# Moving products, a gate and half the stores around in an attention and convolution kernel

## The chip, the core and the metric

The kernel runs on one core of a Trainium2 chip. The metric is the device time of one execution in microseconds, the median over runs. The core has five engines that run side by side, each with its own queue of instructions in a fixed order, and wait for each other by semaphores: TensorE (PE in the profile; its weight loads are shown apart as PEld), VectorE (DVE), ScalarE (ACT), GpSimd (POOL), and SyncE (SP), which only issues DMAs. Matmul results land in PSUM, [...] from which DVE and ACT copy them to SBUF.

## What is computed

The input `x` has 8 images of 64 channels and 64 x 64 pixels. Layer 0 is attention over the 4096 pixels of each image, with an added global (unary) term; layer 1 sums three convolutions (1x1, 3x3, 5x5) of signs with sign weights, each with a batch norm, and multiplies the sum by a gate that is computed from its mean:

```python
# layer 0
q = wq @ xf + bq;  k = wk @ xf + bk;  v = wv @ xf + bv
q = q - q.mean();  k = k - k.mean()          # over the pixels
sim = softmax(q.T @ k / 8)                   # 4096 x 4096 per image
x = x + v @ sim.T + v @ softmax(q_mean @ k)
# layer 1
s = sum(norm_k(conv_k(sign(x + move_k), sign_weights_k)) for k in (1, 3, 5))
gate = sigmoid(grouped(mean(s)) + gb)        # one number per image and channel
out = s * gate + x
```

## The kernel before

Two images form a pair, one on partitions 0 to 63, one on 64 to 127; there are four pairs. Their 4096 queries are cut into NQ = 8 blocks of 512. I call block g the g-th of the 32 blocks; g // 8 is its pair and qb = g % 8 its place in the pair. Each block walks over the 4096 keys in 32 steps of 128 (`attend`, L1057 to L1068). The order of all instructions is written out by hand: what Python calls first stands first in the queue of its engine.

One step j does this. `scores` (L466) issues four f32 matmuls of 64 x 64 x 512 to a score tile `ps` (a pair of banks; the pool has two such tiles, tag "s"), and ACT takes the exponential into a tile `e` (L481). Then, for the step before, `weighted` (L484) multiplies those exponentials by the values and adds into `acc` (one pair of banks, tag "acc"), and `summed` (L497) has DVE add them into `es`, the denominators. After that come the pieces of other work that `plan` (L953) put at step j with `put`; pieces at the same step run in the order of the `put` calls.

At step 0 of a block, between the last weighted sums of the block before and the first ones of the new block, lies what I call the seam. There `weighted_out` (L506) copies `acc` to SBUF (tile `o`), `send` and `gather` (L516, L523) carry `es` through DRAM into a tile `parts` from the pool of exponentials, and `both` (L982) calls `mix_rows` (L862). That function interleaves two sequences of small matmuls, one for each half of the array's rows: the queries of block g + 1 (`pq`, two halves in two "m" banks), and the convolutions of block g - 3. Those are 70 products for the 5x5 (groups S, A, B in one score tile, D in an "m" bank), 24 for the 3x3 (A, B, S, D in the pair of banks "acc") and two 1x1 matmuls. Each entry of a sequence has a length in units (queries 2.0, a product 0.5, the 1x1 1.0), and the two sequences are merged by running position; each entry issues two matmuls. When the queries' matmuls are done, `split_queries_out` (L459) moves them to SBUF; when 5x5 D is done, `begin_rows` (L700) has ACT start the sum tile `sb` from it. At the end `hold_rows` (L729) has ACT copy the 3x3 results to SBUF (`es_z`), and `add_rows` (L715) has DVE add S (two additions), A and B of the 5x5 to `sb`. The held 3x3 results and the 1x1 are added some steps later (`add_held`, `end_rows`).

`fold` (L531) turns the gathered `parts` into reciprocals `rec`, and `spread` (L543) sends them through DRAM to all partitions. `check_block` lets ACT compare them with limits. `added` and `finish` make the layer's output `x2` on DVE, and the `signs` functions put its signs into padded images on ACT.

Once per pair there is more. The next pair's `x` is loaded in its predecessor's block qb = 2; `mean_part` sums it (DVE, quarters), `mean_scores` at block qb = 4 makes from it, with a one-column matmul `pm`, the vectors `mx` and `nmx` that the queries need; `values` and `unary_part` follow in qb = 4 to 7; `unary_end` at the next pair's block 0 has two one-column matmuls `po`. The gate of a pair takes `gate_mean` and `gate` (a one-column matmul `pg`, then ACT and DVE), and `store` multiplies a block of sums by it on DVE and sends it out.

## Time and profile before

| | us |
|---|---|
| median of 3 runs | 1955.12 (1954.63 to 1955.45) |
| the profiled execution, whole | 1956.16 |
| its span in the profile | 1953.9 |
| mean granted TensorE clock | 0.998 |
| ACT exponentials, L481, 1024 of them | 1049.1 busy, 1.025 each |
| DVE additions to `es`, L504, 960 of them | 1173.2 busy, 1.222 each |
| TensorE scores, L470, 8192 records | 1094.8 busy |
| TensorE weighted sums, L489, 8192 records | 1086.7 busy |
| DVE `fold`, L533, 31 of them | 60.7 busy, 1.958 each |

Busy time of TensorE counts the time in which at least one matmul runs; four 64 x 64 matmuls can run at once in the four quarters of the array, and each f32 matmul leaves two records. In the chain that ended last, four such matmuls of 512 columns take 0.86 us together. L12 is line 12 of the kernel. A record such as "L481 ACT ACTIVATE e<-ps" names the line, the engine, the operation, and the tile written and read.

### The profile page before, as it was taken

The page shows a single profiled execution, that of the slowest core. Times are in us where ns is not written, and L with a number is a line of the kernel's source. Part 1 is how long each engine was busy: PE and PEld are TensorE (multiplying, and loading weights), DVE is VectorE, ACT ScalarE, POOL GpSimd, SP SyncE. Part 2 cuts the span into 40 slices and gives each one's busy share as a digit, 9 for nine tenths or more (in the row PEclk, how much of TensorE's full clock was granted, in tenths as well). Part 3 has the DMA queues.
Part 4 walks back from the last instruction along what each step waited for, and adds up shares of the span by engine and source line. Part 5 has one row for each costly group of instructions (what it writes and reads, how often), then busy time and mean ns, then how long its engine had stood idle before and what let it go on. Part 6 is the DMA issues. An engine that isn't in the chain of part 4 may idle for free.

```text
span 1953.9 us, 48347 instructions
## 1 busy us (share of the span) xinstructions
PE 1927.4 (99%) x20848; PEld 810.3 (41%) x20848; DVE 1683.2 (86%) x2077; ACT 1249.1 (64%) x1474; POOL 5.9 (0%) x26
## 2 busy tenths in 40 slices
PE   9999999999999999999999999999999999999997
PEld 4333434443444434444444443344444444444444
DVE  6878988889888899888898888998888888988976
ACT  5666666666666666666666666666666666666663
POOL 0000000000000000000000000000000000000000
PEclk9999999999999999999999999999999999999999
DMA  3021111110102121111101212011111011111111
GB/s 100 31 69 30 27 37 34 40 35 16 40 31 83 37 67 29 37 34 40 34 16 40 74 50 67 20 36 37 34 39 33 17 40 52 62 39 33 28 34 46
DMA packets 58997, 80.57 MB, mean 41 GB/s; under 512 B 15628, under 2 KB 40600, under 8 KB 58648
## 3 DMA queue, kind: packets, MB, share of 16 engines
q1 hardware_dynamic: 58024, 76.22, 12.8%
q8 instruction: 165, 2.70, 0.6%
q10 hardware_dynamic: 720, 1.18, 0.2%
q14 instruction: 56, 0.46, 0.1%
q0 software_dynamic: 32, 0.01, 0.0%
HBM read 39.27 MB, written 24.77 MB: 33 GB/s over the span
## 4 chain that ended last, share of the span: by engine, by line
PE 87%; DVE 6%; ACT 5%; issue 1%; DMA 1%; SPq 0%; DVEq 0%; ACTq 0%
PE acc L489 41%; PE ps L470 40%; DVE es L504 4%; PE z L692 2%; ACT sb L707 1%; ACT es_z L732 1%; ACT e L481 1%; PE pq L455 1%; PE pv L311 1%; PE z L763 1%; DMA e_parts<-es 1%; PE z_5d L692 0%; DVE fold L533 0%; DMA x<-in_x 0%; DVE sb L725 0%
## 5 line engine op out<-in xcount | busy, mean ns | idle before, releaser
L481 ACT ACTIVATE e<-ps 128x1024 f32<-128x1024 f32 x1024 | 1049.1, 1025 | 623.9 <-PE ps L470 584.4
L504 DVE TENSOR_TENSOR es<-es,e 128x1024 f32<-128x1024 f32 x960 | 1173.2, 1222 | 137.9 <-ACT e L481 85.1
L470 PE MATMUL ps<-q,x 64*64 64x512 f32 x8192 | 1094.8, 591 | 0.9 <-DVE kb L165 0.9
L489 PE MATMUL acc<-e,v 64*64 64x512 f32 x8192 | 1086.7, 590 | 7.6 <-ACT e L481 4.6
L489 PEld LDWEIGHTS acc<-e,v 64*64 64x64 f32 x8192 | 325.7, 131 | 570.5 <-ACT e L481 297.6
L470 PEld LDWEIGHTS ps<-q,x 64*64 64x64 f32 x8192 | 348.7, 133 | 501.0 <-issue 271.4
L725 DVE SCALAR_TENSOR_TENSOR sb<-z,frac,sb 128x256 f32<-128x256 f32 x87 | 39.2, 478 | 61.8 <-PE z L692 61.8
L692 PE MATMUL z<-e,wt 64*64 64x256 bf16 x754 | 84.3, 269 | 0.1
L692 PE MATMUL z<-ec,wt 64*64 64x256 bf16 x754 | 84.3, 270 | 0.0
L692 PEld LDWEIGHTS <-wt 64*64 64x64 bf16 x1508 | 76.7, 105 | 1.1 <-issue 0.3
L692 PEld LDWEIGHTS <-wc 64*64 64x64 bf16 x1218 | 67.5, 105 | 2.9 <-issue 0.5
L533 DVE TENSOR_REDUCE fold<-e_parts 128x256 f32<-128x1024 f32 x31 | 60.7, 1958 | 3.6 <-DMA e_parts<-es 3.6
L725 DVE SCALAR_TENSOR_TENSOR sb<-es_z,frac,sb 128x256 f32<-128x256 f32 x145 | 62.2, 479 | 0.0
L692 PE MATMUL z<-ec,wc 64*64 64x256 bf16 x464 | 60.9, 271 | 0.0
L707 ACT ACTIVATE sb<-z_5d,shift,frac 128x256 f32<-128x256 f32 x58 | 29.6, 561 | 41.1 <-PE z_5d L692 41.1
L608 ACT ACTIVATE s<-x,vec 128x512 bf16<-128x512 f32 (+2 forms) x66 | 46.2, 702 | 5.4 <-DVE x L576 5.2
L502 DVE TENSOR_TENSOR es<-e,e 128x1024 f32<-128x1024 f32 x32 | 39.2, 1225 | 8.6 <-ACT e L481 8.6
L692 PE MATMUL z<-e,wc 64*64 64x256 bf16 x319 | 44.8, 271 | 0.0
L462 DVE TENSOR_SCALAR q<-pq,mx 128x256 f32<-128x256 f32 x60 | 27.0, 480 | 15.5 <-PE pq L455 15.0
L511 ACT COPY o<-acc 128x1024 f32<-128x1024 f32 (+2 forms) x33 | 32.3, 981 | 1.2 <-PE acc L489 1.2
L311 PEld LDWEIGHTS pv<-wx,x 64*64 64x64 f32 x1024 | 22.3, 134 | 17.1 <-issue 8.8
L732 ACT COPY es_z<-z 128x1024 f32<-128x1024 f32 x29 | 29.3, 1011 | 0.0
(153 smaller groups left out, 713.8 us busy)
## 6 DMA issues: line engine op xcount, KB each, us to landing
es<-es SPq DMA_DIRECT2D x31, 512.0 KB
e_parts<-es SPq DMA_DIRECT2D x124, 128.0 KB
r<-rc SPq DMA_DIRECT2D x62, 128.0 KB
x<-in_x SPq DMA_DIRECT2D x15, 512.0 KB
out<-sb SPq DMA_DIRECT2D x28, 256.0 KB
ec<-e SPq DMA_DIRECT2D x29, 153.0 KB
xc<-in_x SPq DMA_DIRECT2D x60, 64.0 KB
ec<-e SPq DMA_DIRECT2D x29, 132.0 KB
```

Of the source, the lines that this page charges most:

```text
L311: nc.tensor.matmul(pv[img[h], b, i * w : (i + 1) * w], self.x[img[b], bass.ds((4 * g + i) * P + h * H, H)], self.wx[img[b], :], start=True ...
L470: nc.tensor.matmul(ps[img[h], b, :], self.x[img[b], bass.ds(j * P + h * H, H)], self.q[qb][img[b], :], start=True, stop=neg is None,)
L481: nc.scalar.activation(e, ps, AF.Exp, scale=1.0 / 8.0)
L489: nc.tensor.matmul(self.acc[qb][img[b], h, :], self.v[img[h], j, img[b]], e[img[h], b, :], start=(j == 0), stop=(j == NK - 1),)
L502: nc.vector.tensor_tensor(self.es[qb], self.first, e, ALU.add)
L504: nc.vector.tensor_tensor(self.es[qb], self.es[qb], e, ALU.add)
L533: nc.vector.tensor_reduce(f, self.parts.rearrange("p g c -> p c g"), AX.X, ALU.add)
L608: nc.scalar.activation(sy[n][0][:, rows, pad : pad + HH], self.x2[qb][:, r0 * HH : r1 * HH].rearrange("p (h w) -> p h w", w=HH), AF.Sign, ...
L692: nc.tensor.matmul(z[img[b], :].rearrange("p (h w) -> p h w", w=HH), taps[img[h], c * C : c * C + C], src[:, first : first + 3 * step + 1 ...
L707: nc.scalar.activation(sv[:, :, t, :], z.rearrange("p (j w) -> p j w", w=HH), AF.Identity, bias=shift, scale=frac[5][:, t : t + 1],)
L725: nc.vector.scalar_tensor_tensor(out, z.rearrange("p (j w) -> p j w", w=HH), by, out, ALU.mult, ALU.add)
L732: nc.scalar.copy(self.z3, two)
```

## The change

- In `mix_rows` the order of the products changes. Before, the first sequence was 5x5 S, 3x3 A, the 1x1, 3x3 B, S, D, and the second 5x5 A, D, B. Now the first is eight of S, all 3x3, the last two of S, the 1x1, and the second six of A, all D, the last four of A, B. `hold_rows` is called when 3x3 D is done, no longer after all products.
- `both` is put ahead of `mean_scores`, `unary_end` and `mean_rows_out` at step 0.
- Half the queries' results go to SBUF on ACT in place of DVE.
- `gate` moves from step 0 of block qb = 3 to step 13 of qb = 2, `gate_mean` from step 20 to 11; four of the eight `store` calls of a pair move to block qb = 2, and the others start at step 12 of qb = 3 with 4 steps between them, in place of step 3 with 3 between.
- The means of the next pair are taken in eight parts on ACT in place of four on DVE.
- `fold` is cut into `fold_first`, `fold` and `fold_last` at steps 3, 4, 5: two additions of halves in place of one reduction over four. `spread`, `add_held`, `end_rows`, `added` and `finish` move one to four steps later.
- The pool of exponentials (and `parts`) has five buffers in place of four. Room comes from smaller scratch tiles, the tile `rc` used for the fold too, and nine sum tiles `sb` in place of ten.

```diff
-    ep = ctx.enter_context(tc.tile_pool(name="ep", bufs=4))
+    ep = ctx.enter_context(tc.tile_pool(name="ep", bufs=5))
...
-                junk = ep.tile([P, N // 4], F32, tag="e", name=f"mean_{self.name}_{c}")
+                junk = sm.tile([P, N // 4], BF16, tag="cl", name=f"mean_{self.name}_{c}")
...
-            for h, c in enumerate(SPLIT):
-                nc.vector.tensor_scalar(
-                    q[:, c], self.pq[h][:, 0 : c.stop - c.start], self.mx, None, ALU.subtract
-                )
+            data = [self.pq[h][:, 0 : c.stop - c.start] for h, c in enumerate(SPLIT)]
+            nc.vector.tensor_scalar(q[:, SPLIT[0]], data[0], self.mx, None, ALU.subtract)
+            nc.scalar.activation(q[:, SPLIT[1]], data[1], AF.Identity, bias=self.nmx)
...
+        def fold_first(self, qb):
+            two = [self.parts[:, 2 * i : 2 * i + 2, :] for i in range(2)]
+            nc.vector.tensor_tensor(two[0], two[0], two[1], ALU.add)
+            self.rc = self.tile(fp, "rc", qb, (P, QB // 2))
+
         def fold(self, qb):
-            f, t = self.tile(fp, "fold", qb, (P, QB // 2)), self.parts[:, 0, :]
-            nc.vector.tensor_reduce(f, self.parts.rearrange("p g c -> p c g"), AX.X, ALU.add)
+            parts, f, t = self.parts, self.rc, self.parts[:, 0, :]
+            nc.vector.tensor_tensor(f, parts[:, 0, :], parts[:, 1, :], ALU.add)
             nc.vector.transpose(out=t, in_=f)
+
+        def fold_last(self, qb):
+            t = self.parts[:, 0, :]
             nc.vector.tensor_reduce(
                 rec, t.rearrange("p (k i) -> p k i", i=32), AX.X, ALU.add
             )
             nc.vector.reciprocal(rec, rec)
...
+        def sum_tile(self, qb):
+            return bp.tile([P, QB], F32, tag="sb", bufs=9, name=f"sb_{self.name}_{qb}")
...
-            seqs[0] += products(5, "S") + products(3, "A") + [((1,), 0, 1.0)]
-            seqs[0] += products(3, "B") + products(3, "S") + products(3, "D")
-            seqs[1] += products(5, "A") + products(5, "D") + products(5, "B")
+            S, A = products(5, "S"), products(5, "A")
+            three = [t for name in "ABSD" for t in products(3, name)]
+            seqs[0] += S[:8] + three + S[8:] + [((1,), 0, 1.0)]
+            seqs[1] += A[:6] + products(5, "D") + A[6:] + products(5, "B")
...
+            elif left[n] == 0 and n == (3, "D"):
+                p.hold_rows(qb, z3)
         if c is not None:
-            p.hold_rows(qb, z3)
             for n in "SAB":
                 p.add_rows(qb, 5, n, z[5, n])
...
-            if qb == 3 and pr >= 1:
-                put(0, pairs[pr - 1].gate)
+            put(0, both)
             if qb == 4 and pr + 1 < n_pairs:
-                put(0, lambda: nx().mean_scores())
+                put(0, lambda: nx().mean_scores(8))
...
-            put(0, both)
             if g >= 3:
                 p3, b3 = block(g - 3)
-                put(4, p3.add_held, b3, "AB")
-                put(6, p3.add_held, b3, "SD")
-                put(8, p3.end_rows, b3)
+                put(7, p3.add_held, b3, "AB")
+                put(8, p3.add_held, b3, "S")
+                put(9, p3.add_held, b3, "D")
+                put(10, p3.end_rows, b3)
             if g >= 1:
-                put(3, p.fold, b)
-                put(5, p.spread, b)
+                put(3, p.fold_first, b)
+                put(4, p.fold, b)
+                put(5, p.fold_last, b)
+                put(6, p.spread, b)
...
-                put(10, p.added, b)
-                put(12, p.finish, b)
+                put(12, p.added, b)
+                put(13, p.finish, b)
...
-                put(20, pairs[pr - 1].gate_mean)
-            if qb == 3 and pr >= 1:
-                for i in range(NQ):
-                    put(3 + 3 * i, pairs[pr - 1].store, i, rows_of(pr - 1))
+                put(11, pairs[pr - 1].gate_mean)
+                put(13, pairs[pr - 1].gate)
+            if qb in (2, 3) and pr >= 1:
+                for i in range(NQ // 2):
+                    put((15, 12)[qb - 2] + 4 * i, pairs[pr - 1].store, NQ // 2 * (qb - 2) + i, rows_of(pr - 1))
...
-                    for c in range(4):
-                        put(14 + 4 * c, lambda c=c: nx().mean_part(c, quarters[c]))
+                    for c in range(8):
+                        cols = slice(c * QB, (c + 1) * QB)
+                        put(14 + 2 * c, lambda c=c, cols=cols: nx().mean_part(c, cols, True))
```

## The prediction

> **What bounds the kernel now.** I read the page first, then the order of instructions in time at one ordinary seam (the stretch between two blocks, step 0 of a block), then the waits, then the starts of all 1024 exponentials.

> From the page, busy time and the chain that ended last:

> ```profile
> PE 1927.4 (99%) x20848; PEld 810.3 (41%) x20848; DVE 1683.2 (86%) x2077; ACT 1249.1 (64%) x1474; POOL 5.9 (0%) x26
> ...
> PE 87%; DVE 6%; ACT 5%; issue 1%; DMA 1%; SPq 0%; DVEq 0%; ACTq 0%
> ```

> TensorE is the bound. In mid-block nothing else shows: exponentials start every 1.717 us (605.58, 607.30, 609.01), which is the 0.86 us of scores plus 0.86 us of weighted sums in the chain. So what the change can win are the places where an exponential starts later than 1.717 us after the one before. A plain block takes 58.58 us (1028.57 to 1087.15): 32 x 1.717 = 54.95, and 3.63 at its seam. Blocks with two `values` take 1.02 more (59.60), TensorE's own work. Beyond these: block 1 (58.35 us, with no convolution in its seam), block 2 (57.42, likewise), block 4 (62.83, so 3.23 extra), blocks 11, 19, 27 (61.25, 2.67 extra), 12 and 20 (61.11, 1.51 extra), 8, 16, 24 (59.83, 1.25 extra). The ends of these blocks are in step; nothing else is lost but start and tail, which the change leaves alone.

> The seam of block 10 in order of time (start, length, engine, line; in brackets the idle time before and who ended it):

> ```profile
> 609.93 1.01 ACT L511 COPY o<-acc 128x1024 f32<-128x1024 f32 x1
> ...
> 610.28 0.88 DVE L462 TENSOR_SCALAR q<-pq,mx 128x256 f32<-128x256 f32 x2 [0.70 <-PE pq L455]
> ...
> 611.97 1.02 ACT L707 ACTIVATE sb<-z_5d,shift,frac 128x256 f32<-128x256 f32 x2 [1.03 <-PE z_5d L692]
> ...
> 612.93 1.01 ACT L732 COPY es_z<-z 128x1024 f32<-128x1024 f32 x1
> 613.14 0.88 DVE L725 SCALAR_TENSOR_TENSOR sb<-z,frac,sb 128x256 f32<-128x256 f32 x2 [1.99 <-PE z L692]
> 613.93 0.47 DVE L725 SCALAR_TENSOR_TENSOR sb<-z,scale,sb 128x256 f32<-128x256 f32 x1
> ...
> 614.00 0.21 PEld L489 LDWEIGHTS acc<-e,v 64*64 64x64 f32 x8 [1.00 <-ACT es_z L732]
> ...
> 614.33 0.47 DVE L725 SCALAR_TENSOR_TENSOR sb<-z,frac,sb 128x256 f32<-128x256 f32 x1
> 614.92 0.24 PEld L470 LDWEIGHTS ps<-q,x 64*64 64x64 f32 x8 [0.71 <-issue]
> ```

> Two waits end this seam nearly together. The weighted sums need the bank pair of the 3x3 products, which `hold_rows` copies out (until 613.94; they start at 614.00). The scores of step 2 need the score banks that the 5x5 products S, A, B lay in. DVE's four additions empty them at 614.80, and the scores' weights load at 614.92, 0.06 us after the weighted sums would have let them anyway (614.00 + 0.86). The first addition starts at 613.14 although S ended some 1.5 us earlier and ACT's first `sb` at 612.53: in the built order its wait on PE names the last product of the seam (the last of B, ended at 613.03), in both kernels, because S, A and B share one tile.

> The waits that the special blocks add (total us, times, longest):

> ```profile
> PEld acc L489 <- ACT es_z L732: 28.3, 29, 1.0
> ...
> ACT e L481 <- DVE es L504: 16.9, 20, 1.3
> ...
> ACT e L481 <- DVE rec L535: 8.1, 6, 2.6
> ...
> PEld pq L455 <- ACT gt L802: 2.7, 3, 0.9
> PE pm L288 <- DVE xm L286: 2.7, 3, 1.5
> ```

> 28.3 us is the size of the prize as the waits show it; the seam above says it is not to be had.

> [...] weights of the weighted sums load at 615.40 for matmuls at 615.83. [...] The one-column matmuls pm, po, pg are 128*128 between 64*64 work; in block 12 pm takes 0.31 us (730.23 to the queries at 730.54), so I charge 0.3 to 0.4 each.

> **The change, part by part.**

> *3x3 ahead, `hold_rows` earlier (28 seams with queries, one without).* TensorE has the same 94 products and the same 1x1; the longer of the two sequences still has 14.5 units of 0.22 us, so z ends no earlier. In the new order 3D ends near 612.6 and `hold_rows` near 613.65, so the weighted sums can follow the scores (612.85 + 0.86 = 613.7). But the additions still start 0.11 us after the last B and end 1.66 us later, so the scores of step 2 still load 1.89 us after z ends. Gain: nothing, at most 0.09 (614.95 against 614.86).

> *The D products come earlier.* They write the bank of the first query half and wait for DVE's q (610.28 + 0.48 = 610.76, some 0.05 to 0.1 more until PE sees it). Before, 42 products stood ahead of them (611.19, no wait). Now 26 do: at four per 0.107 us from 610.04 they are due at 610.73. A stall of 0.1 to 0.17, plus up to 0.1 until the four tiles run evenly again. No row shows it; below nothing is excluded, as z cannot end earlier; above, 0.35 if pipelines refill slowly. I take 0.18, and all of it shows, since the additions hang on the end of z: 28 x 0.18 = **+5.0** (0 to +9.8). The 3x3 products, due 0.16 later, then find the copy of `o` done (610.94). ACT's half of q lies at 610.9 to 611.4, before `sb`, and its bank is wanted last, by the 1x1: nothing. DVE's saved 0.4 lies in its idle 1.99.

> *Gate and stores.* Blocks 11, 19, 27 lose 1.57 in the seam (pq waits for gt, behind `o` on ACT) and 1.06 in steps 9 to 18, where eight stores of 0.74 put DVE behind until four buffers of exponentials are full. DVE needs about 1.31 per addition there (eight in 10.52 us), so it has only 0.41 us free per step. The gate goes to step 13 of the block before: ga is ready (end_rows and then one addition, some 2 us before), gt on ACT falls after an exponential, cost 0.4 for pg. Four stores go to block 10, from which 4 x 1.21 of means leave; four stay, from step 12. The fold costs DVE about 0.68 + 0.36 in place of 1.96, and there is a fifth buffer, so the 1.06 goes. 3 x (0.4 - 2.67) = **-6.8** (-8 to -4).

> *Means on ACT.* Eight of 0.61 + 0.19 (row L274), about 0.71 of ACT's sequence each; ACT has 1.717 - 0.92 free per step, and signs (0.71) sit there already without delaying an exponential. Nothing; if one spills over, 0.1 each, 32 of them, +3 at most.

> *Small matmuls behind the seam.* `mean_scores`: xm now stands on DVE behind the four additions, so pm starts about 1.9 after z ends and the scores of step 1 wait for it; step 2's scores then start at z + 3.97 instead of z + 1.92, 2.05 extra. Before: 1.51 twice (xm was late behind DVE's backlog, 730.10), 3.23 in block 4, of which 0.78 was a fold. 2 x 0.54 - 1.18 = **-0.1**. `unary_end`: two matmuls, 0.65, then ACT's two checks wait for su behind the additions and delay exponential 1, so the sums of step 1 come 0.95 late against 1.25: 3 x -0.3 = **-0.9**. Behind the waiting pm and po stand all of TensorE's scores; that is priced.

> *Fold in steps, fifth buffer.* In blocks 1 and 2 exponential 5 waited for rec (1.86 and 0.82, some given back: 1.5 and 0.5 net), because the fold waits for its DMA (1.76 in block 1). In the new order the buffer that the fold frees is wanted by exponential 8, 5 us later. With the first po behind the queries (0.5) and nmb (0.25): **-2.75**.

> *SP and memory.* Store DMAs move on SP ahead of the copies of rows, which have 13 steps until used; nine sum buffers suffice, as each reused one was stored a block before. Nothing.

> Sum: 5.0 - 6.8 - 0.1 - 0.9 - 2.75 = -5.55. The profiled execution has a span of 1953.9 and took 1956.16; so 1948.35 and 1950.6. The median shown is 1955.12, 1.04 below the profiled one: **1949.6 us**, -0.28%. About 0.2% (3.9 us) is what a measurement here can tell from no change.

> **Rivals.** (a) Forecast, the additions' chain hides the earlier copy, the D wait is small: 1946 to 1951.1, chance 0.43. (b) The D wait costs as much as the special blocks give, 0.3 to 0.38 per seam, or spilled means add 3: 1953.5, no measurable change, 0.25. For it: q ends just where D is due. Against: no refill seen so far is longer than 0.1. (c) D doesn't wait at all, or the 0.09 of the tie is had too: 1955.1 - 10.6 = 1944.5 (1942 with the tie), 0.12. For it: PE's times are modelled to about 0.1. Against: DVE's end is a record. (d) Slower: the D matmul, waiting for DVE's q at the head of TensorE's queue, drains all four tiles, and each seam loses 0.6 before they stream again: 16.8 - 10.55 = +6.2, 1961.4, chance 0.20. It breaks even at 0.38 a seam and is slower by 0.2% from 0.52. For it: everything in the seam stands behind that one matmul. Against: weights can load meanwhile.

> (e) That the change does what it says for the 3x3 wait, 0.4 x 29 = 12 us more, I count as no case of its own: the wait on the last B excludes it.

> Faster 0.55 (a, c), same 0.25 (b), slower 0.20 (d). The range takes in (a), (c), (b) and (d) up to half a microsecond a seam: 1943.5 to 1958.5, leaving out the rest of (d) and (c) with the tie.

> **What would show it.** Right: the wait of acc for es_z is gone and a wait of ps for DVE's `sb` stands in its place; ordinary blocks take 58.6 to 58.9 us; D's first product starts right after q; blocks 11, 19, 27 near 59.2, blocks 12 and 20 longer than 61.2; no wait of e for rec. Wrong: plain blocks at 58.2 or below (the additions start before B ends), or above 59.1 (the D wait is large), or exponentials late in steps 14 to 28 of blocks 3, 10, 18, 26 (the means).

## The result and the profile after

The changed kernel takes 1951.48 us (median of 4 runs, 1950.84 to 1954.38), the kernel before 1955.28 beside it; the ratio is 0.9983, with a 95% interval from 0.9966 to 1.0000. So this comparison alone can't tell the change from none; the kernel with four buffers, which has the same block lengths, gives 0.9983 (0.9976 to 0.9990) in 18 executions below, and that can. The profiled execution of the changed kernel took 1954.38 with a span of 1952.2. It is the longest of the four: in it the first exponential starts at 17.10 us, in the one of before at 15.04. The other kernels below, all with the same start, lie between 14.5 and 17.1, so these 2 us are no part of the change. I therefore compare from the first to the last exponential: 1909.72 before, 1906.19 after.

From the page of the changed kernel, busy time and the chain that ended last:

```profile
PE 1923.2 (99%) x20848; PEld 800.4 (41%) x20848; DVE 1617.6 (83%) x2066; ACT 1275.4 (65%) x1552; POOL 5.9 (0%) x26
...
PE 94%; DVE 3%; ACT 1%; issue 1%; DMA 0%; DVEq 0%; SPq 0%
```

DVE lost 66 us of work (fold, means, half of q), and the share of DVE and ACT together in the chain fell from 11% to 4%. The time has hardly moved all the same. The waits of the changed kernel (total us, times, longest):

```profile
PEld acc L491 <- ACT es_z L744: 11.7, 23, 0.6
...
PE pm L288 <- DVE xm L286: 5.9, 3, 2.0
...
ACT ck L416 <- DVE su L366: 4.8, 4, 1.5
PE ps L472 <- DVE sb L737: 4.5, 23, 0.2
```

The wait for the copy of the 3x3 results fell from 28.3 us to 11.7, the one for gt is gone, and no exponential waits for `rec`. New are a wait of `ps` for the additions, 0.2 in each of 23 seams, three waits of `pm` for `xm` of 2.0 each, and waits of ACT's check for `su`, as forecast for `unary_end`.

Block lengths, from the starts of the exponentials in the two profiled executions, say where the time went:

| block | before | after |
|---|---|---|
| plain (9, 17, 25) | 58.58 | 58.68 |
| with `values` (5 to 7 and so on) | 59.60 | 59.72 |
| 1 | 58.35 | 56.94 |
| 2 | 57.42 | 57.03 |
| 10, 18, 26 | 58.58 | 59.15 |
| 11, 19, 27 | 61.25 | 58.68 |
| 4 | 62.83 | 63.47 |
| 12 | 61.11 | 63.47 |
| 20 | 61.11 | 61.76 |
| 8, 16, 24 | 59.83 | 59.42 |

An ordinary seam grew by 0.11 us. The seam of block 18 in the changed kernel (order of time; start, length, engine, line; in brackets the idle time before and who ended it):

```profile
1089.48 1.01 ACT L513 COPY o<-acc 128x1024 f32<-128x1024 f32 x1
1089.83 0.48 DVE L465 TENSOR_SCALAR q<-pq,mx 128x256 f32<-128x256 f32 x1 [0.70 <-PE pq L458]
1090.37 0.27 PE L701 MATMUL z_5d<-e,wc 64*64 64x256 bf16 x1
...
1091.15 1.02 ACT L719 ACTIVATE sb<-z_5d,shift,frac 128x256 f32<-128x256 f32 x2 [0.28 <-PE z_5d L701]
...
1092.10 1.01 ACT L744 COPY es_z<-z 128x1024 f32<-128x1024 f32 x1
...
1092.77 0.88 DVE L737 SCALAR_TENSOR_TENSOR sb<-z,frac,sb 128x256 f32<-128x256 f32 x2 [2.46 <-PE z L701]
1093.17 0.33 PEld L491 LDWEIGHTS acc<-e,v 64*64 64x64 f32 x8 [0.52 <-ACT es_z L744]
...
1093.96 0.47 DVE L737 SCALAR_TENSOR_TENSOR sb<-z,frac,sb 128x256 f32<-128x256 f32 x1
...
1094.55 0.24 PEld L472 LDWEIGHTS ps<-q,x 64*64 64x64 f32 x8 [1.05 <-PE ps L472]
1094.58 1.09 PE L472 MATMUL ps<-q,x 64*64 64x512 f32 x8 [0.20 <-DVE sb L737]
```

D's first product starts 0.06 after DVE's q has ended (1090.31). ACT has `sb` first and takes the 3x3 copy as soon as it is free; the copy ends at 1093.11 and the weighted sums go. They end at about 1094.4, the last addition at 1094.43, and the scores of step 2 load at 1094.55 and start at 1094.58, after 0.20 in which TensorE stood idle. The earlier copy is there, and the additions end the seam as before.

What I had not priced stands in the seam of block 12 in the changed kernel: the four additions, the reduction `xm` behind them on DVE, `pm`, which waits for `xm`, and what TensorE does after that:

```profile
732.05 0.88 DVE L737 SCALAR_TENSOR_TENSOR sb<-z,frac,sb 128x256 f32<-128x256 f32 x2 [2.45 <-PE z L701]
...
733.63 0.15 DVE L286 TENSOR_REDUCE xm<-xs 128x1 f32<-128x8 f32 x1
...
733.93 0.35 PE L288 MATMUL pm<-xm,mm 128*128 128x1 f32 x2 [1.96 <-DVE xm L286]
...
734.21 1.81 PE L472 MATMUL ps<-q,x 64*64 64x512 f32 x8
...
735.77 1.95 PE L491 MATMUL acc<-e,v 64*64 64x512 f32 x8
```

The eight records of scores take 1.81 us; in an ordinary seam they take 1.09. The windows of the same kernel (stretch, sum, busy time of PE, PEld, DVE, ACT and POOL with counts, then the granted clock, DMA share, GB/s) show why; the last two are the same place in block 20:

```profile
732.00:734.00 2.00, 0.07 (x1) 0.10 (x1) 1.73 (x5) 0.39 (x1) 0.00 (x0) 1.00 0.41 122
734.00:736.00 2.00, 2.00 (x14) 0.89 (x18) 0.67 (x5) 0.00 (x0) 0.00 (x0) 0.61 0.65 191
736.00:738.00 2.00, 2.00 (x14) 0.58 (x12) 0.88 (x1) 1.02 (x1) 0.00 (x0) 0.53 0.04 14
738.00:740.00 2.00, 2.00 (x24) 0.76 (x20) 0.51 (x2) 1.03 (x1) 0.00 (x0) 1.00 0.00 0
1211.00:1213.00 2.00, 0.54 (x6) 0.51 (x10) 1.46 (x8) 0.00 (x0) 0.00 (x0) 1.00 0.84 247
1213.00:1215.00 2.00, 2.00 (x24) 0.63 (x20) 0.56 (x6) 1.02 (x1) 0.00 (x0) 1.00 0.28 83
```

Behind an idle time of 1.96 us the clock of TensorE stood near half for some 3.4 us, in blocks 4 and 12 but not in 20, and each time this cost 1.71 us (63.47 against 61.76) on top of the wait. I call these 3.4 us a slow stretch. The experiments take the parts one by one.

### The profile page after: what moved, and what is told of

Same layout as the page of the kernel before. It is cut to its first block, busy times and chain, and to the rows that moved or that the text cites. A ratio compares the mean times of both kernels' runs of the same rounds, so it can differ in the third digit from the quotient of the medians.

```text
span 1952.2 us, 48415 instructions
## 1 busy us (share of the span) xinstructions
PE 1923.2 (99%) x20848; PEld 800.4 (41%) x20848; DVE 1617.6 (83%) x2066; ACT 1275.4 (65%) x1552; POOL 5.9 (0%) x26
## 3 DMA queue, kind: packets, MB, share of 16 engines
q10 hardware_dynamic: 720, 1.18, 0.2%
## 4 chain that ended last, share of the span: by engine, by line
PE 94%; DVE 3%; ACT 1%; issue 1%; DMA 0%; DVEq 0%; SPq 0%
PE ps L472 44%; PE acc L491 44%; PE z L701 3%; DVE sb L737 2%; PE pv L311 1%; PE pq L458 1%; PE z_5d L701 1%; PE z L775 1%; ACT e L483 0%; DMA x<-in_x 0%; PE warm L155 0%; DVE es L506 0%; DVE r L574 0%; DMA out<-sb 0%; PE pq L430 0%
## 5 line engine op out<-in xcount | busy, mean ns | idle before, releaser
L472 PEld LDWEIGHTS ps<-q,x 64*64 64x64 f32 x8192 | 338.9, 133 | 516.1 <-PE ps L472 259.6
L701 PEld LDWEIGHTS <-wc 64*64 64x64 bf16 x1218 | 62.6, 106 | 6.7 <-issue 0.5
L701 PE MATMUL z<-ec,wc 64*64 64x256 bf16 x464 | 60.9, 271 | 0.0
L504 DVE TENSOR_TENSOR es<-e,e 128x1024 f32<-128x1024 f32 x32 | 39.2, 1225 | 17.8 <-ACT e L483 17.8
L465 DVE TENSOR_SCALAR q<-pq,mx 128x256 f32<-128x256 f32 x30 | 14.5, 484 | 20.7 <-PE pq L458 20.7
L701 PE MATMUL z<-s,wc 64*64 64x256 bf16 x145 | 26.3, 275 | 0.0
```

What stands on the lines that cost most here:

```text
L472: nc.tensor.matmul(ps[img[h], b, :], self.x[img[b], bass.ds(j * P + h * H, H)], self.q[qb][img[b], :], start=True, stop=neg is None,)
L504: nc.vector.tensor_tensor(self.es[qb], self.first, e, ALU.add)
L701: nc.tensor.matmul(z[img[b], :].rearrange("p (h w) -> p h w", w=HH), taps[img[h], c * C : c * C + C], src[:, first : first + 3 * step + 1 ...
```

## The experiments

My theory before them: a seam ends by the additions, which wait for the last B; the new order gives nothing and costs the 0.11 that it grew; the loss in blocks 4 and 12 is a wait that makes TensorE idle and an idle time that slows its clock. The first rival: the order does what it is for, and something else eats the gain. The second: the clock falls there for another reason than the wait.

**The old order in the changed kernel.**

```diff
-            seqs[0] += S[:8] + three + S[8:] + [((1,), 0, 1.0)]
-            seqs[1] += A[:6] + products(5, "D") + A[6:] + products(5, "B")
+            seqs[0] += products(5, "S") + products(3, "A") + [((1,), 0, 1.0)]
+            seqs[0] += products(3, "B") + products(3, "S") + products(3, "D")
+            seqs[1] += products(5, "A") + products(5, "D") + products(5, "B")
...
-            elif left[n] == 0 and n == (3, "D"):
-                p.hold_rows(qb, z3)
         if c is not None:
+            p.hold_rows(qb, z3)
```

> The changed kernel with the old order of the products and the 3x3 results held at the end of the seam again; all else stays. If the four additions on DVE behind the last B set the end of the seam, and the order only brings the wait of D: the seam shrinks by the 0.11 us that it grew, 28 x 0.11 = 3.1 us less than the changed kernel's 1951.5, so 1948.4; plain blocks back at 58.6, the wait of acc for es_z back at about 28 us. If the change of order did what it is for, and something else ate the gain: about 28 x 0.4 = 11 us more, 1962.5.

Measured: 1949.95 (ratio to before 0.9976, 0.9966 to 0.9986). Plain blocks take 58.57, and in its waits stands again

```profile
PEld acc L491 <- ACT es_z L744: 23.8, 26, 1.0
```

So 12 us of waiting for the copy come back and each seam gets 0.11 shorter. The rival is out: the wait that the reorder halves was worth nothing, since TensorE would have waited for the additions anyway.

**Only D later.**

```diff
-            seqs[1] += A[:6] + products(5, "D") + A[6:] + products(5, "B")
+            seqs[1] += A + products(5, "D") + products(5, "B")
```

> The changed kernel with 5x5 D behind all ten A again, so that 42 products or nearly stand ahead of it, and the 3x3 products still ahead. If the 0.11 us that each seam grew is the wait of D for DVE's q: plain blocks 58.58, about 3 us less than the changed kernel, 1948.4. If it is something else in the new order (the copies, the changes between groups): plain blocks stay at 58.69 and the time at 1951.5.

Measured: 1951.23 (0.9980, 0.9972 to 0.9988), too coarse to tell. The blocks tell it: plain ones 58.62 to 58.64. Of the 0.11 some 0.05 is D's early place and the other 0.06 stays with the rest of the order. Neither expectation was quite right.

**xm a block earlier.**

```diff
+        def mean_sum(self, parts):
+            self.xm = self.tile(sm, "xm", 0, (P, 1))
+            nc.vector.tensor_reduce(self.xm, self.xs[:, 0:parts], AX.X, ALU.add)
...
+                if qb == 3:
+                    put(31, lambda: nx().mean_sum(8))
```

> The changed kernel with the reduction xm done at the last step of block qb = 3, so that pm need not wait for DVE's additions. If the wait makes the idle time of TensorE and the idle time lowers its clock: blocks 4, 12 and 20 fall from 63.5, 63.5 and 61.8 to about 60.0, that is 3 x 1.7 for the wait and twice 1.7 for the clock, 8.5 us in all: 1943.0, and the granted clock stays near full at these seams. If the clock falls for another reason at this place (the change of shape of the matmuls, the work ahead): the wait goes, the clock still falls: 1946.4.

Measured: 1942.72 (0.9937, 0.9923 to 0.9950), as the theory said. Blocks 4, 12 and 20 take 59.75, 59.77 and 59.76, no more than 0.05 above a block with `values`, and the granted clock is 1.00 in all windows from 252 to 262 us. So `pm` behind the seam is free once nothing makes it wait: its 0.35 lies beside the additions. The five runs lie within 0.5 us of each other, where 14 runs of the kernel with D later are spread over 5.4; a slow stretch that comes in some seams of some executions would give that.

**A shorter wait.** xm stands between the second and the third addition.

```diff
             for n in "SAB":
                 p.add_rows(qb, 5, n, z[5, n])
+                if n == "S" and between is not None:
+                    between(8)
```

> The changed kernel with the reduction xm placed between the second and the third of the four additions in the seam of block qb = 4, so that TensorE waits for it about 1.97 - 0.9 = 1.1 us. If the clock falls only behind a wait near 2 us: blocks 4, 12 and 20 all take 61.76 - 0.9 = 60.9 and none shows a slow stretch: 1951.5 - 2.6 x 2 - 0.9 = 1945.4. If any wait of TensorE at this place can lower the clock: two of the three take 1.7 more: 1948.8.

Measured: 1946.99 (0.9962, 0.9949 to 0.9976). Its seam of block 12 in order of time, and the windows there:

```profile
727.74 0.15 DVE L286 TENSOR_REDUCE xm<-xs 128x1 f32<-128x8 f32 x1
...
728.03 0.35 PE L294 MATMUL pm<-xm,mm 128*128 128x1 f32 x2 [1.18 <-DVE xm L286]
...
728.32 1.09 PE L478 MATMUL ps<-q,x 64*64 64x512 f32 x8
```

```profile
726.00:728.00 2.00, 0.85 (x27) 0.58 (x17) 1.05 (x4) 1.28 (x2) 0.00 (x0) 1.00 0.24 68
728.00:730.00 2.00, 1.97 (x18) 0.96 (x22) 1.25 (x7) 0.53 (x1) 0.00 (x0) 1.00 0.68 218
730.00:732.00 2.00, 2.00 (x24) 0.76 (x20) 1.23 (x1) 1.31 (x2) 0.00 (x0) 1.00 0.14 43
```

TensorE waits 1.18 to 1.20 in the three seams, the scores behind take 1.09, the clock stays at 1.00, and the blocks take 61.00, 60.99 and 60.98. The price of the shorter wait alone is left. The median lies 1.6 above the first expectation all the same and 1.8 below the second; the profiled execution took 1946.10, and the other four, 1946.62 to 1948.61, have no profile.

**The small matmuls ahead of the seam again.** Nothing else is undone.

```diff
-            put(0, both)
             if qb == 4 and pr + 1 < n_pairs:
                 put(0, lambda: nx().mean_scores(8))
...
+            put(0, both)
             if g >= 3:
```

> The changed kernel with the queries and products put behind the small matmuls again in blocks 0 and 4 of a pair. If the order behind the seam is what makes TensorE idle for 2 us and then slow: blocks 4, 12 and 20 take about 61.2 to 61.5 with a wait of pm for xm ahead of the seam and no slow stretch, blocks 8, 16 and 24 0.4 more: 1951.5 - 2.1 x 2 - 0.4 + 1.2 = 1948.1. If the wait of pm is as long ahead of the seam as behind it (1.5 against 1.96) and the clock falls there too: about 1951.

Measured: 1945.69 (0.9953, 0.9939 to 0.9967). Blocks 4, 12 and 20 take 60.45, blocks 8, 16 and 24 take 59.83 (0.41 more than in the changed kernel). Blocks 1 and 2, with the first `po` and the row means, take 56.77 and 56.87, that is 0.18 and 0.16 less. The loss ahead of the seam is now only 0.73 (60.45 - 59.72), where before it was 1.51 and more: with the means off DVE and a shorter fold, `pm` finds xm done. This part of the change undid some 6 us of what the other parts had won.

**Gate and stores back.**

```diff
+            if qb == 3 and pr >= 1:
+                put(0, pairs[pr - 1].gate)
...
-                put(11, pairs[pr - 1].gate_mean)
-                put(13, pairs[pr - 1].gate)
+                put(20, pairs[pr - 1].gate_mean)
+            if qb == 3 and pr >= 1:
+                for i in range(NQ):
+                    put(3 + 3 * i, pairs[pr - 1].store, i, rows_of(pr - 1))
```

> The changed kernel with gate, gate_mean and the eight stores where they were before (gate in the seam of block qb = 3, stores from step 3, three steps apart). If the stall in steps 9 to 18 of blocks 11, 19, 27 went because the fold is cut and a fifth buffer is there, it stays away and only the wait of pq for gt returns: 3 x (1.57 - 0.46) = 3.3 us more than the changed kernel's 1951.5, so 1954.8, blocks 11, 19, 27 near 60.3 and 10, 18, 26 at 58.7. If it went because the stores moved, it returns too: 3 x 1.06 more, 1958.0, blocks 11, 19, 27 near 61.3.

Measured: 1953.99 (0.9995, 0.9987 to 1.0003). Blocks 11, 19 and 27 take 60.32 (1.64 more), blocks 10, 18 and 26 take 58.67 (0.48 less): 3 x 1.16 = 3.5 us. The stall of 1.06 beside the stores does not return; moving four of them was not what removed it.

**Four buffers; the old fold with five; the old fold with four.** In the second and third the fold is one reduction over four again, all of it at step 3, and `spread` at step 5. The first edit below is that of the first and third, the others those of the second and third.

```diff
-    ep = ctx.enter_context(tc.tile_pool(name="ep", bufs=5))
+    ep = ctx.enter_context(tc.tile_pool(name="ep", bufs=4))
...
-            two = [self.parts[:, 2 * i : 2 * i + 2, :] for i in range(2)]
-            nc.vector.tensor_tensor(two[0], two[0], two[1], ALU.add)
...
-            nc.vector.tensor_tensor(f, parts[:, 0, :], parts[:, 1, :], ALU.add)
+            nc.vector.tensor_reduce(f, parts.rearrange("p g c -> p c g"), AX.X, ALU.add)
...
-                put(4, p.fold, b)
-                put(5, p.fold_last, b)
-                put(6, p.spread, b)
+                put(3, p.fold, b)
+                put(3, p.fold_last, b)
+                put(5, p.spread, b)
```

> The changed kernel with four buffers of exponentials. If the fifth buffer is what lets the fold stand two steps later: exponential 5 of every block waits for fold_last, which stands behind the addition of exponential 4, some 0.9 us late in each of 31 blocks, about 25 us more, 1976. If the fold's place does not matter in ordinary blocks, and the fifth buffer helps only in blocks 1 and 2: 2 us more, 1953.5.

> The changed kernel with the fold as before (one reduction over four, all of it at step 3, spread at step 5) and five buffers. If the later place of the fold, or a fifth buffer, either of them, is enough to keep the exponentials of blocks 1 and 2 from waiting: blocks 1 and 2 stay at 56.9 and 57.0 and the time at 1951.5. If the long reduction at step 3 is what makes them wait, buffers or not: they return to 58.35 and 57.4, 1.8 us more, 1953.3.

> The same with four buffers. If the place of the fold is what helped and the fifth buffer does nothing beside it: blocks 1 and 2 return to about 58.35 and 57.4, as exponential 5 again takes the buffer that the fold frees: 1.8 us more than the changed kernel, 1953.3, with a wait of e for rec again. If neither fold nor buffers did it, but the means or what else left DVE: they stay at 56.9 and 57.0.

Measured: 1951.89 (0.9983, 0.9976 to 0.9990), 1953.55 (0.9990, 0.9982 to 0.9999) and 1953.25 (0.9993, 0.9984 to 1.0001). With four buffers, and with the old fold and five, blocks 1 and 2 stay at 56.94 and 57.03. With both undone block 1 takes 57.72 and block 11 takes 59.04 (0.36 more), and in its waits stands again

```profile
ACT e L483 <- DVE rec L543: 3.7, 3, 1.8
```

So one of the two was enough, and the pair is worth 1.1 us. The 25 us that I expected of four buffers were wrong. Which exponential takes the buffer that the fold frees can be read in the traces, as it is the one that waits for the DMAs of `gather` and `spread`: exponential 5 of a block with the old fold and four buffers, 6 with the old fold and five, 7 with the later fold and four, 8 in the changed kernel. With four buffers I had expected exponential 5, and 7 comes late enough not to wait. Blocks 1 and 2 had lost 0.63 (58.35 - 57.72) and 0.39 (57.42 - 57.03) more in the kernel before, and which other part took that away was not tried. Nor do the blocks show why the median with the old fold and five buffers is 2 us above the changed kernel's: from first to last exponential its profiled execution has 1906.17. Slow stretches in more of its other executions would do it (13 runs, 1950.5 to 1955.1), but that is argued, not shown.

**A shorter chain at the end of the seam.** The products of S, A and B, which share the score tile, come first and D last; DVE starts `sb` from S and adds D at the end.

```diff
-                nc.scalar.activation(
+                nc.vector.tensor_scalar(
                     sv[:, :, t, :],
                     z.rearrange("p (j w) -> p j w", w=HH),
-                    AF.Identity,
-                    bias=shift,
-                    scale=frac[5][:, t : t + 1],
+                    frac[5][:, 0:1],
+                    shift,
+                    ALU.mult,
+                    ALU.add,
                 )
...
-            seqs[0] += S[:8] + three + S[8:] + [((1,), 0, 1.0)]
-            seqs[1] += A[:6] + products(5, "D") + A[6:] + products(5, "B")
+            seqs[0] += S + three + [((1,), 0, 1.0)]
+            seqs[1] += A + products(5, "B") + products(5, "D")
...
-            elif left[n] == 0 and n == (5, "D"):
-                p.begin_rows(qb, z[n])
+            if n[0] == 5 and n[1] in "SAB" and sum(left[5, m] for m in "SAB") == 0:
+                p.begin_rows(qb, z[5, "S"])
+                for m in "AB":
+                    p.add_rows(qb, 5, m, z[5, m])
...
-            for n in "SAB":
-                p.add_rows(qb, 5, n, z[5, n])
+            p.add_rows(qb, 5, "D", z[5, "D"])
```

> The changed kernel with the 5x5 groups S, A, B done first and D last, and sb begun by DVE from S (ACT's two operations from D go, DVE has two more), so that the four additions that empty the score tile start some 0.55 us before the products end and D's two follow. If the chain last product, additions, scores of step 2 sets the end of the seam: it ends where the scores and sums of steps 0 and 1 let it, some 0.2 us earlier, and D no longer waits, 0.11: 28 x 0.25 to 0.3 = 7 to 8 us less, plain blocks near 58.4; blocks 4, 12 and 20 0.3 longer, as xm stands behind six additions: about 1944.5. If the additions are not what ends the seam: only the wait of D goes, 1948.4, or nothing, 1951.5.

Measured: 1951.58 (0.9980, 0.9973 to 0.9988), the changed kernel's time. Its seam of block 18 in order of time, from the first addition to the scores of step 2, and then the end of its seam of block 16:

```profile
1089.12 0.99 DVE L719 TENSOR_SCALAR sb<-z,frac,shift 128x256 f32<-128x256 f32 x2 [1.73 <-PE z L701]
...
1090.42 0.47 DVE L738 SCALAR_TENSOR_TENSOR sb<-z,frac,sb 128x256 f32<-128x256 f32 x1
...
1090.95 0.15 PEld L472 LDWEIGHTS ps<-q,x 64*64 64x64 f32 x4 [0.36 <-DVE sb L738]
```

```profile
969.76 0.86 DVE L738 SCALAR_TENSOR_TENSOR sb<-z_5d,frac,sb 128x256 f32<-128x256 f32 x2
...
970.77 0.35 PE L361 MATMUL po<-ones,vu 128*128 128x1 f32 x2 [2.20 <-DVE sb L738]
```

The seam did what was expected: DVE starts while D still runs, and every plain block takes 58.28, 0.40 less than in the changed kernel, 11 us over 28 seams. But the bank of D stays taken until DVE has added it, and `po` needs that bank: TensorE waits 2.20, and blocks 8, 16 and 24 take 61.08, 62.78 and 62.78 in place of 59.42. The last two have the slow stretch again (clock 0.65 and 0.50 from 972 to 976 us). These three blocks took 8.4 us more than in the changed kernel, and so most of the 11 us.

**Both put together.** Seam as in the last run but with the 3x3 products two of S earlier, xm early, `pm` at step 8 of its block and `po` at step 11, where TensorE does not stand idle for them; then the same with all ten S ahead of the 3x3 and `po` of block 1 back in its seam. Beside the edits above, the second has

```diff
-                put(0, lambda: nx().mean_scores(8))
-                put(0, lambda: nx().mean_scores_out())
-                put(1, lambda: nx().value_weights())
+                put(8, lambda: nx().mean_scores(8))
+                put(8, lambda: nx().mean_scores_out())
+                put(9, lambda: nx().value_weights())
...
-                put(0, pairs[g // NQ].unary_end)
-                put(0, pairs[g // NQ].unary_out)
+                put(0 if g == 1 else 11, pairs[g // NQ].unary_end)
+                put(0 if g == 1 else 11, pairs[g // NQ].unary_out)
```

> The changed kernel with the 5x5 groups S, A, B ahead of D and sb begun from S on DVE, the 3x3 products two of S earlier so that their copy ends in time, xm at the end of block qb = 3, and the small matmuls pm and po with what follows them at steps 8 and 11, where a bank is free. If the end of the seam was the additions' chain and then the copy of the 3x3 results: seams shorter by 0.40 + 0.14, 28 x 0.54 = 15 us; blocks 4, 12 and 20 at the length of a block with values plus 0.46, 7.2 us less; blocks 8, 16 and 24 0.3 less each: 1951.5 - 15 - 7.2 - 0.9 = 1928.4. If the copy is not what holds the sums now: 28 x 0.14 = 4 us more, 1932.3.

> The kernel of the run best with the order of the run release (all ten S ahead of the 3x3) and po of block 1 in its seam again. If the seam is 58.28 long in this order and 58.34 in the other: 28 x 0.06 + 0.5 = 2.2 us less than 1934.9, 1932.7. If the two orders differ by something else of the run release: 1934.4.

Measured: 1934.85 (0.9896, 0.9881 to 0.9911) and 1931.95 (0.9884, 0.9869 to 0.9899). From the page of the second:

```profile
PE 97%; DVE 1%; ACT 1%; DMA 0%; issue 0%; SPq 0%; DVEq 0%
```

Moving the 3x3 ahead of the last S gave nothing: plain blocks take 58.34 with it and 58.28 without, so the copy did not hold the sums, and of the 6.5 us by which the first missed its forecast 5.3 are 28 x 0.19 of that. The second beats both kernels of this case: 1.16% less than before, with plain seams of 3.3 us (58.28 - 54.95) and blocks 4, 12 and 20 at 59.78. Its four runs lie within 0.4 us.

The waits near 2 us, counted over all kernels with the seam of the changed one (it, the old order, D later, gate and stores back, and the three with fold and buffers): 21 waits of 1.96 to 1.99 us, 14 of them with a block near 63.4, the other 7 near 61.8. In the run with the shorter chain 3 of 6 waits of 2.20 to 2.27 lowered the clock. Of the three waits of 1.2, and the one of 1.46 in block 4 of the kernel before (clock 1.00 there), none did.

## Why the prediction was right or wrong

The time came out near, 1949.6 for 1951.48, and the change is small and faster as forecast, though 0.17% is less than what I had said a measurement here can tell from no change. Of the mechanism most was right and one term failed. That the sum came so near is luck in part: the terms of `mean_scores` (3.4 too low) and of the fold (0.95) were offset by those of D (1.9 too high) and of `unary_end` (0.7), and the slow stretches in it come in some seams and not in others. The time lies 0.4 above the range of case (a), whose mechanism it is; the outcome of case (b), a change too small to tell, came without its cause.

- *3x3 ahead, nothing gained*: right, shown by the old order, and it excludes the case (e) that I had set aside. That the copy would end early enough for the wait to vanish was wrong: ACT's `sb` comes before it, and 11.7 of 28.3 us of that wait stayed, hidden.
- *D, 0.18 a seam, +5.0*: the mechanism is there, the size was too large. The seam grew by 0.11, 3.1 us in all, and D's place is about half of that; the refill after the wait costs nothing that can be seen. Cases (b) and (d) are out; the 0.35 for a slow refill and the 0.6 of case (d) were estimates of mine that no trace shows.
- *Gate and stores, -6.8*: measured 3 x (0.57 - 0.11 - 2.57 - 0.11) = -6.7, the seams' growth taken out. `pg` costs 0.48 in mid-block (0.4 taken). The gate and the stores by themselves are worth 3.5 of it, as the run with both back shows; the stall went with other parts, of which only 0.36, in block 11, can be put down to fold and buffer. The 59.2 that I named for blocks 11, 19 and 27 does not follow from this term, which puts `pg` a block earlier: blocks 10, 18 and 26 take 59.15.
- *Means on ACT, nothing*: right; no exponential of steps 14 to 28 comes late.
- *Small matmuls: mean_scores, -0.1*: this step failed. The wait was right: block 20 loses 2.04 in its seam (61.76 - 59.72), where I had 2.05. Two things were missing. The idle time lowers the clock, 1.71 in each of two blocks. And I priced against the waits of before, though the rest of the change takes DVE's backlog away and with it half of what `pm` cost ahead of the seam (0.73). Measured against before: 0.64 + 2.36 + 0.65 less three times the 0.11 gives +3.3. Half the clock for 3.41 us is what the trace shows (256.58 to 259.99 and 734.45 to 737.86), each time behind 1.96 to 1.98 us of idle time with 1.4 us of work in the same 3.41 us (last section). I had not asked what an idle time of 2 us does.
- *unary_end, -0.9*: measured 3 x (-0.41 - 0.11) = -1.6, again with the seams' growth taken out.
- *Fold and fifth buffer, -2.75*: -1.8 in blocks 1 and 2 (1.41 and 0.39), of which only 0.78, in block 1, can be put down to fold and buffer. The 0.75 that I gave to the first `po` and `nmb` behind the queries had the wrong sign: putting them ahead again made the two blocks 0.34 shorter. That exponential 5 waited there for `rec` was right, as the wait returns with the old fold and four buffers; that this wait was all that these blocks lost was not.

The sum of what was measured, 3.1 - 6.7 + 3.3 - 1.6 - 1.8 = -3.7, stands against -3.5 from the first to the last exponential. Without the two slow stretches of the profiled execution the change would have come to about -7, an estimate (3.5 + 2 x 1.71).

## What to carry to other kernels

Ask of every instruction that waits at the head of TensorE's queue how long the engine then stands idle: here 2 us of idle time cost up to 1.7 us more afterwards, and reducing one small vector a block earlier was worth 8.8 us. A wait in the list is no prize while a second chain ends at the same time; find what releases the tile (the score tile by four additions behind the last product) and shorten that. Count an edit against the kernel that the other edits leave, not against the one before.

## What was not expected of the hardware

Whether it comes differs between seams of the same execution. In the profiled one of the changed kernel the granted clock is 0.50 four times: from 7.41 to 10.82 us, from 256.58 to 259.99 behind the wait of block 4, from 734.45 to 737.86 behind that of block 12, and from 1942.77 to the end. The starts lie 249.17, 477.87 and 1208.32 us apart; divided by 73, 140 and 354 that gives 3.413 us each time, the length of one stretch. These are the windows of that length, counted from those starts, around blocks 4, 12 and 20, two for each block, in the form used above:

```profile
253.17:256.58 3.41, 1.43 (x18) 0.66 (x15) 2.39 (x10) 0.67 (x1) 0.00 (x0) 1.00 0.45 140
256.58:259.99 3.41, 3.41 (x22) 1.05 (x18) 1.23 (x1) 1.02 (x1) 0.00 (x0) 0.50 0.20 57
...
731.03:734.45 3.42, 1.46 (x36) 1.17 (x30) 1.86 (x7) 1.36 (x2) 0.00 (x0) 1.00 0.35 105
734.45:737.86 3.41, 3.41 (x20) 1.07 (x16) 1.27 (x6) 1.02 (x1) 0.00 (x0) 0.50 0.29 87
1208.86:1212.27 3.41, 1.64 (x56) 1.36 (x45) 1.68 (x5) 1.97 (x3) 0.00 (x0) 1.00 0.44 121
1212.27:1215.68 3.41, 3.22 (x30) 1.42 (x34) 1.43 (x7) 1.09 (x2) 0.00 (x0) 1.00 0.33 100
```

In blocks 4 and 12 one window holds the whole wait (1.98 and 1.96 us without a matmul in it), and the next window runs at clock 0.50. In block 20 the border at 1212.27 cuts the wait, 1.77 us without a matmul ahead of it and 0.19 behind it, and the clock stays at 1.00. That the place of a wait between such borders decides whether the clock falls is my reading of these three waits; it is not shown beyond them.

The late start of the changed kernel's profiled execution may be the same: its clock is 0.50 from 7.41 to 10.82 us, and its first exponential starts at 17.10; in the execution of before the clock is 1.00 from 5 to 12 us, and the first exponential starts at 15.04.
